# Two transformer layers on one core: one plan for both layers, with shared places in memory

## The chip, the cores and the metric

The kernel runs on one core of a Trainium2 chip. The metric is the device time of one execution, in microseconds (us); it is measured several times, and the median counts.

## The reference

The input is 128 sequences of 64 tokens with 128 features, with a context of the same shape. Two layers follow each other. Layer 0 of the reference is a cross attention with 16 heads and then a routed attention with 8 experts, layer 1 a decoder block and then a mixture of 16 experts:

```python
x = x + _L0_xattn_ref(_layernorm(x), ctx_1024, ...)      # softmax(q k^T / sqrt(8)) v, 16 heads
x = x + _L0_ffn_ref(_layernorm(x), Wr, Wqkv, Wo)         # per expert: top 8 of 64 tokens, rotary q and k, causal softmax
x = x + _L1_xattn_ref(_layernorm(x), ctx_1024, ...)      # self attention, norm, cross attention, norm, relu FFN, norm
x = x + _L1_ffn_ref(_layernorm(x), router_w, bias, ...)  # 4 of 16 experts by group, silu(h) * u, plus 2 shared ones
```

The text below calls the first two lines layer 1 of the kernel, and the last two lines layer 2, as the kernel does ("first_layer", "second_layer"). All is computed in float32.

## The kernel before

The 8192 tokens are cut into 16 chunks of 512 (8 sequences). A chunk lies in SBUF as four tiles of 128 tokens by 128 features, and its transpose as 128 features by 512 tokens, which is one PSUM bank.

Nothing is issued directly. A layer is recorded operation by operation into a `Plan`, by recorders for VectorE (V), ScalarE (A), GpSimd (G), TensorE (T) and the DMA queue of SyncE (Y). `Plan.run` then orders it: it keeps a clock for each engine, takes durations from its own table (`duration`), and always places the operation that can start first, with ties broken by a rank made of the chunk number times a pace, less the length of the work behind it. A chunk may run at most `window` chunks ahead of the oldest unfinished one. Buffers have a tag and a number of slots, and an operation that writes a new buffer has to wait for a slot. In the end all operations are issued in the planned order, so that each engine works strictly through its own list. Almost every instruction carries line 337 (350 after the change), the line that issues them, so a profile is read by the names of tiles.

Before the change there are two plans. `first_layer` opens its pools, records all 16 chunks, runs the plan and closes its pools; then `second_layer` does the same. The two exchange the stream x through DRAM tiles `xm`. Layer 2's weights are fetched when its plan begins. The names that matter:

- Layer 1, each chunk: `x` and `cT` (the context, transposed by the host) come by DMA; LayerNorm gives `z`, TensorE turns it into `zT` (through `tr_ps`); `psk`, `psq`, `psv` are the projections; then an attention in two halves. Each half has sixteen score products `pss`, sums `sc`, a row maximum `mx` that GpSimd subtracts, four transposes `pst`, four exponentials `e` and the products `pso` with the values; `psa` turns the result, `psw` is the output projection.
- Layer 1, each pair of chunks (`routed_attention`): `psl` gives the router's logits, `lg` their sigmoid; they go through DRAM (`logits_d`, `rows`, `rows_d`, `psr`), VectorE ranks them, and one-hot matrices (`hot`, `hotT`) gather (`psg`) and scatter (`psz`) the tokens. At the start the value and output weights of each expert are multiplied into one matrix, `wvo` (the fold: `wvT_ps`, `wvo_ps`).
- Layer 2, each chunk: `decoder_block` has two attentions of the same kind, LayerNorms into z0 to z3, and residual tiles r0 to r3 (`moved` scales and shifts them on GpSimd); `ph` and `po` are the FFN. `expert_layer` routes (`r_psl`, `psc`), sends the combination weights through DRAM so that each partition gets them (`comb_d`, `all_w`), and runs 18 experts: `gate`, `up`, Silu into `mo_g`, times `all_w` on GpSimd, times `up` on VectorE into `mo_a`, and `y`, which accumulates over all experts.

PSUM has eight banks: four ("a") for scores and `pso`, and four ("m") for all else; in layer 2 three of these are "m" and one holds `y`.

Of the kernel before, what the change touches and what calls it, by code (L numbers as in the profile page):

```python
# [25 lines left out]
P = 128  # L26
# [14 lines left out]
PACE1 = 25  # L41
# [22 lines left out]
C_M4, C_BM, C_RK, C_COS, C_SIN, C_TRI, C_R8, C_END = 0, 4, 132, 134, 198, 262, 518, 526  # L64
# [80 lines left out]
class Op:  # L145
    def __init__(self, n, engine, chunk):
        self.n, self.engine, self.chunk = n, engine, chunk
        self.calls, self.us, self.late, self.mode = [], 0.0, 0.1, None
        self.deps, self.then, self.waits, self.ready, self.start, self.end = set(), [], 0, 0.0, 0.0, 0.0
        self.bufs, self.news, self.line_up, self.done = [], [], [], False  # L150


class Plan:
# [3 lines left out]
    def __init__(self, tc, window, prompt=(), pace=0):  # L157


        self.prompt, self.pace = prompt, pace  # L160
        self.tc, self.nc, self.window = tc, tc.nc, window
        self.ops, self.chunk, self.group = [], 0, None
        self.tags, self.turns = {}, {}
        nc = tc.nc
        self.V, self.A, self.G, self.T, self.Y = (
            Recorder(self, e, n) for e, n in ((nc.vector, "V"), (nc.scalar, "A"), (nc.gpsimd, "G"), (nc.tensor, "T"), (nc.sync, "Y"))
        )

    def new(self, pool, shape, name, slots=None, dtype=F32, tag=None, in_turn=False):

        tag = name if tag is None else tag
        slots = pool.slots[tag] if isinstance(pool, Banks) else slots
# [7 lines left out]
    def held(self, tile):  # L180

        return View(Buf(None, list(tile.shape), None, None, 0, None, tile), np.broadcast_to(np.int8(0), list(tile.shape)))
# [20 lines left out]
    def _add(self, calls, us):  # L203
# [22 lines left out]
        for b, reads, writes in seen.values():  # L226
            if reads or writes:
                op.deps.update(b.writers)
            if writes:
# [9 lines left out]
            op.bufs.append(b)  # L239
        op.deps.discard(op)  # L240
# [3 lines left out]
    def free_slots(self, b):  # L244
        return self.tags.setdefault((id(b.pool), b.tag), [0.0] * b.slots)
# [8 lines left out]
    def run(self):  # L254
# [6 lines left out]
        for op in reversed(ops):  # L261
            op.tail = op.us + op.late + max((x.tail for x in op.then if x.chunk == op.chunk), default=0.0)
            op.rank = op.chunk * self.pace - op.tail if self.pace else op.n
# [7 lines left out]
        while done < len(ops):  # L271
# [27 lines left out]
            for b in op.news:  # L299
                slots = self.tags[id(b.pool), b.tag]  # L300
                b.slot = min(range(len(slots)), key=lambda s: slots[s])
                slots[b.slot] = math.inf
# [13 lines left out]
            for b in op.bufs:  # L316
                b.left -= 1
                b.free_at = max(b.free_at, op.end)
                if not b.left and b.slot is not None:
                    self.tags[id(b.pool), b.tag][b.slot] = b.free_at  # L320
            cand[op.engine].remove(op)
            for x in op.then:
                x.ready = max(x.ready, t + us if x.engine == op.engine and op.engine != "Y" else op.end)
# [9 lines left out]
        for op in order:  # L333
            for b in op.news:
                b.real = b.pool.tile(b.shape, b.dtype, name=b.name, tag=f"{b.tag}.{b.slot}", bufs=1)
# [3 lines left out]
        self.ops, self.tags = [], {}  # L339
# [12 lines left out]
def duration(engine, method, out, args, kw):  # L352
# [10 lines left out]
    if engine == "Y":  # L363
        return 0.1, 2.5 + n * out.shadow.shape[0] * 5.0e-6 * 4, None
# [10 lines left out]
    return 0.1 + n * (0.0023 if len(whole) > 1 and min(map(elements, whole)) == n else 0.0019), 0.1, None  # L375

@with_exitstack
def two_layers(ctx: ExitStack, tc: tile.TileContext, a: dict, out: bass.AP):
# [15 lines left out]
    mats = const.tile([P, len(MATS), P], F32, name="mats")  # L394
    nc.scalar.dma_start(out=mats, in_=a["mats"].rearrange("m i o -> i m o"))
    mat = {n: mats[:, i, :] for i, n in enumerate(MATS)}
    rows_t = const.tile([P, len(ROWS), P], F32, name="rows_t")
    nc.scalar.dma_start(out=rows_t, in_=a["rows"].unsqueeze(0).to_broadcast([P, len(ROWS), P]))
    row = {n: rows_t[:, i, :] for i, n in enumerate(ROWS)}
# [12 lines left out]
    def normed(pl, src, sb, affine=False, role="", n=3):  # L412
# [20 lines left out]
        z = pl.new(sb, [P, T, P], "z", n, tag="z" + role)  # L433
# [21 lines left out]
    class Attention:  # L455
# [10 lines left out]
        def __init__(self, pl, pool, ps, n_v, n_kx, s, t, o="o"):  # L466

            one = pool("at1")
            self.pl, self.sb, self.ps, self.n_kx, self.s, self.t, self.o = pl, pool("at2"), ps, n_kx, s, t, o

            v_bd = [one.tile([P, NB, NP, 2 * V1], F32, name=f"v_bd{i}", tag=f"v_bd{i}") for i in range(n_v)]
            for t in v_bd:
                nc.gpsimd.memset(t, 0.0)
                nc.gpsimd.memset(t[:S, :, :, HD : HD + 1], 1.0)
                nc.gpsimd.memset(t[S:, :, :, V1 + HD : V1 + HD + 1], 1.0)
            self.v_bd = [pl.held(t) for t in v_bd]

# [6 lines left out]
        def run(self, c, zT, kvT, w, resid, dst, mask=None, role=""):  # L484
            names = ("Wq", "Wk", "Wv", "Wo") if w == "L0_xattn_" else ("wq", "wk", "wv", "wo")
            wq, wk, wv, wo = (mat[w + n] for n in names)
# [3 lines left out]
            m = lambda shape, name: pl.new(ps, shape, name, tag="m")  # L490
# [31 lines left out]
            for n in range(2):  # L522

                pss = [pl.new(ps, [P, 2, NR, S], "pss", tag=g) for g in self.s]
                sc = [pl.new(sb, [P, 2, NR, S], "sc", 8) for g in range(NR)]
                pst = [pl.new(ps, [P, 4, P], "pst", tag=self.t) for i in range(4)]
                e = [pl.new(sb, [P, 4, P], "e", 4) for i in range(4)]
                pso = pl.new(ps, [P, 2, NH, V1], "pso", tag=self.o)
# [42 lines left out]
                psa = pl.new(ps, [P, 2, P], "psa", tag=self.t)  # L571
# [12 lines left out]
    def biases(m, raw):  # L584
        nc.vector.tensor_copy(m, raw)
        nc.vector.tensor_scalar(m, m, 0.0, NEG, ALU.is_equal, ALU.mult)

    def query_key_mask(pool, src):

        raw = pool.tile([P, S], I32, name="qk_raw")  # L590
        for j in range(2):
            nc.sync.dma_start(out=raw[j * S : (j + 1) * S], in_=src)
        m = pool.tile([P, S], F32, name="qk_m")
        biases(m, raw)
        return lambda t: m.unsqueeze(1).unsqueeze(1).to_broadcast([P, 2, NR, S])

    def key_mask(pl, sb, c, src):
# [6 lines left out]
        pl.V.tensor_copy(m, raw)  # L604
        pl.V.tensor_scalar(m, m, 0.0, NEG, ALU.is_equal, ALU.mult)
# [3 lines left out]
    def first_layer():  # L609

        with ExitStack() as st:
            pool = lambda name, bufs=1, **kw: st.enter_context(tc.tile_pool(name=name, bufs=bufs, **kw))
            one, sb = pool("fl1"), pool("fl2")
            ps = banks(pool, a=4, m=4)
            pl = Plan(tc, 4, prompt="m", pace=PACE1)
            attend = Attention(pl, pool, ps, 2, 2, ("a",) * NR, "m", "a")
            routed = routed_attention(pl, one, sb, ps, pool("fl_d", space=DRAM))
            xs = []
            for c in range(NCH):
                pl.chunk = c  # L620
                xs.append(pl.new(sb, [P, T, P], "x", 6))
                pl.Y.dma_start(out=xs[c], in_=a["x"][c])
                cT = pl.new(sb, [P, CH], "cT", 3)
                pl.Y.dma_start(out=cT, in_=a["ctxT"][c])
                zT = turned(pl, normed(pl, xs[c], sb, n=2), sb, ps, "m")
                pl.G.tensor_tensor(xs[c], xs[c], over_t(row["L0_xattn_bo"]), ALU.add)
                attend.run(c, zT, cT, "L0_xattn_", xs[c], xs[c])
                if c % 2:
                    routed(c - 1, xs[c - 1 :])
            pl.run()  # L630

    def routed_attention(pl, one, sb, ps, dram):
# [9 lines left out]
        wqkv = one.tile([P, E0, 3 * P], F32, name="wqkv")  # L642
        nc.sync.dma_start(out=wqkv, in_=a["L0_ffn_Wqkv"].rearrange("e i j -> i e j"))
        wo = one.tile([P, E0, P], F32, name="ra_wo")
# [447 lines left out]
```

## Time and profile before

| | us |
|---|---|
| median of three runs | 2141.91 (2139.83 to 2142.22) |
| the profiled execution | 2143.89 |
| its span, from first to last instruction | 2142.1 |
| TensorE busy in it | 1947.6 |
| VectorE, ScalarE, GpSimd busy | 1273.5, 1203.7, 1154.8 |
| layer 1's last result stored | 557.2 |
| first product of layer 2 | 580.7 |

The profile comes from one execution under the hardware profiler. Its page has, among other things, each engine's busy time, the span in 40 slices (a digit is the busy share in tenths, and the row PEclk the granted TensorE clock in tenths), and groups of instructions. An answer on a group or a wait can be asked for any stretch of time. A line of a timeline reads: start, duration, engine, line of the kernel, operation, tile written from tiles read, shape, count, and in brackets the idle time before it with what ended it. A wait for several semaphores is put down to the one that came last, which need not be the one that mattered. A float32 matrix product shows as two records.

### The profile page before, as it was taken

The numbers are of one execution on the slowest core, as the hardware profiler recorded it, in microseconds if no ns is written. First come the engines' busy times: TensorE is split into PE (matmuls) and PEld (weight loads), VectorE is DVE, ScalarE is ACT, GpSimd is POOL, SyncE is SP. The second block draws the span as 40 slices with busy tenths as digits, with TensorE's granted clock in tenths as the row PEclk, the third lists the DMA queues.
The fourth block names the chain that finished last, engine by engine and source line by source line (L and its number), as shares of the span: only waits on it lengthen the run. The fifth ranks groups of instructions, "written<-read, shape, count | busy, mean of one in ns | idle before, by whom it ended". The sixth has DMA issues, their size and how long they took to land. (4 is left out here: it accounts for less than half of the span.)

```text
span 2142.1 us, 41746 instructions
## 1 busy us (share of the span) xinstructions
PE 1947.6 (91%) x16032; PEld 1212.7 (57%) x16032; DVE 1273.5 (59%) x3393; ACT 1203.7 (56%) x2147; POOL 1154.8 (54%) x1332
## 2 busy tenths in 40 slices
PE   6988889887388899999999999999999999999999
PEld 4676666665266655555555555555555555555544
DVE  4567767774477846646565665646465665645442
ACT  5867878865245436464655546465555646554322
POOL 5545555643256645646555565656455555644533
PEclk8999999998689889999999999999999999999999
DMA  4011011100400102021111112021111102111131
GB/s 127 9 42 36 20 43 43 43 21 26 136 4 17 51 33 70 28 87 51 58 51 47 51 47 78 21 97 51 47 51 47 63 35 71 51 55 50 49 110 50
DMA packets 62839, 110.77 MB, mean 52 GB/s; under 512 B 17968, under 2 KB 31792, under 8 KB 62640
## 3 DMA queue, kind: packets, MB, share of 16 engines
q1 hardware_dynamic: 58704, 104.69, 14.7%
q10 hardware_dynamic: 3936, 3.41, 0.6%
q8 instruction: 127, 2.08, 0.4%
q14 instruction: 72, 0.59, 0.1%
HBM read 98.37 MB, written 9.70 MB: 50 GB/s over the span
## 5 line engine op out<-in xcount | busy, mean ns | idle before, releaser
L337 POOL TENSOR_TENSOR sc<-sc,mx 128x512 f32<-128x512 f32 x384 | 394.9, 1051 | 338.6 <-DVE mx L337 330.8
L337 POOL TENSOR_TENSOR mo_g<-mo_g,all_w 128x512 f32<-128x512 f32 x256 | 325.0, 1269 | 204.0 <-ACT mo_g L337 203.8
L337 DVE TENSOR_TENSOR mo_a<-mo_g,up 128x512 f32<-128x512 f32 x288 | 196.4, 682 | 305.5 <-PE up L337 275.4
L337 ACT ACTIVATE mo_g<-gate 128x512 f32<-128x512 f32 x288 | 171.5, 596 | 354.7 <-PE gate L337 352.2
L337 PE MATMUL up<-zT,wu 128*128 128x512 f32 x576 | 310.9, 622 | 6.9 <-ACT mo_g L337 6.9
L337 PE MATMUL gate<-zT,wg 128*128 128x512 f32 x576 | 301.6, 606 | 15.9 <-ACT mo_g L337 14.1
L337 ACT ACTIVATE e<-pst 128x512 f32<-128x512 f32 x384 | 219.5, 598 | 168.0 <-PE pst L337 162.2
L337 PE MATMUL y<-mo_a,wd 128*128 128x512 f32 x576 | 299.1, 601 | 0.0
L337 PEld LDWEIGHTS pso<-v_bd,e 128*64 128x64 f32 x6144 | 216.7, 146 | 129.2 <-issue 63.3
L337 PE MATMUL pst<-ident,sc 128*128 128x128 f32 x1536 | 242.9, 296 | 28.6 <-ACT mo_g L337 9.3
L337 DVE TENSOR_REDUCE mx<-sc 128x8 f32<-128x512 f32 x384 | 245.3, 675 | 37.1 <-ACT sc L337 34.1
L337 PE MATMUL pso<-v_bd,e 128*64 128x18 f32 x6144 | 245.5, 219 | 12.2 <-ACT e L337 9.9
L337 ACT ACT_TABLE_LOAD x160 | 205.3, 1283 | 68.5 <-PE pst L337 59.6
L337 PEld LDWEIGHTS pst<-ident,sc 128*128 128x128 f32 x1536 | 183.6, 150 | 82.2 <-issue 27.2
L337 POOL TENSOR_TENSOR ln_rs<-ln_mv,powers 128x4 f32<-128x4 f32 x112 | 61.4, 553 | 213.6 <-DVE ln_mv L337 178.5
L337 PEld LDWEIGHTS gate<-zT,wg 128*128 128x128 f32 x576 | 104.1, 194 | 116.4 <-issue 81.1
L337 PEld LDWEIGHTS y<-mo_a,wd 128*128 128x128 f32 x576 | 101.6, 190 | 96.4 <-issue 94.6
L337 PEld LDWEIGHTS up<-zT,wu 128*128 128x128 f32 x576 | 99.6, 193 | 95.2 <-issue 66.1
L337 DVE RECIPROCAL rc<-pso 128x32 f32<-128x32 f32 x96 | 34.1, 355 | 175.1 <-PE pso L337 174.8
L337 PE MATMUL pss<-kx,q 32*64 32x256 f32 x3072 | 126.2, 413 | 9.5 <-DVE q L337 3.8
L337 ACT ACTIVATE z<-x,ln_off,ln_rs 128x128 f32<-128x128 f32 x256 | 113.1, 487 | 29.5 <-POOL ln_off L337 29.2
L337 DVE TENSOR_TENSOR sc<-pss,qk_m 128x512 f32<-128x512 f32 x128 | 82.3, 683 | 51.6 <-PE pst L337 26.1
(162 smaller groups left out, 2925.3 us busy)
## 6 DMA issues: line engine op xcount, KB each, us to landing
all_w<-comb_d SPq DMA_DIRECT2D x128, 512.0 KB, 4.4
cT<-in_ctxT SPq DMA_DIRECT2D x32, 256.0 KB, 2.7
x<-in_x SPq DMA_DIRECT2D x16, 256.0 KB, 7.5
psr<-rows_d SPq DMA_DIRECT2D x128, 32.0 KB, 2.1
xm<-x SPq DMA_DIRECT2D x16, 256.0 KB, 2.0
x<-xm SPq DMA_DIRECT2D x16, 256.0 KB, 4.0
out<-x SPq DMA_DIRECT2D x16, 256.0 KB, 2.3
k_raw<-in_mask_Bx1x1xS_if SPq DMA_DIRECT2D x32, 64.0 KB, 2.7
```

What stands on the lines that cost most here:

```text
L337: made = getattr(eng, method)(*map(put, args), **{k: put(v) for k, v in kw.items()})
```

## The change

Both layers are now recorded into one plan, over one pool of SBUF tiles and one set of PSUM banks. A table `PLACES` says which place in memory a tag of layer 2 uses: the experts' weights `wg`, `wu`, `wd` take the places of layer 1's `xg` and `wqk`, `mo_g` and `mo_a` those of small tiles of the routed attention, and so on. Some tags have fewer slots: `e` three instead of four, the routed attention's `zT`, `hot`, `scT`, `y` one instead of two; the plan's window is 5 throughout. In the decoder block LayerNorm writes into the tile that it reads (`dst=r`), `moved` works in place, and one tag `r` with four places carries the stream through all stages, where nine tiles (z0 to z3, r0 twice, r1 to r3) did before.

What holds layer 2 back is written out. Each of its operations gets 100 added to its rank (`BEHIND`). `marks` remembers operations of layer 1: the two first decoders may begin once the logits of pair six (counted from zero) have been sent to DRAM, those of chunks 2 to 5 once the last pair's have; the experts' weights follow the last gather of layer 1. The first four matrices and the first row are fetched at once, the other eight and nine with layer 2's weights, all now on SyncE's queue, and the routed attention's weights come after the first two chunks' x. `duration` charges a DMA 0.4 us on the queue instead of 0.1.

The diff, cut to its core:

```diff
-PACE1 = 25
+BEHIND = 100
+EARLY = 6
+WINDOW = 5
...
-            op.rank = op.chunk * self.pace - op.tail if self.pace else op.n
+            op.rank = op.chunk * self.pace - op.tail + op.behind if self.pace else op.n
...
-        return 0.1, 2.5 + n * out.shadow.shape[0] * 5.0e-6 * 4, None
+        return 0.4, 2.2 + n * out.shadow.shape[0] * 5.0e-6 * 4, None
...
+PLACES = {
+    "kx0": ["kx.0"], "kx1": ["kx.1"], "q0": ["q.0"], "q1": ["q.1"], "aT0": ["aT.0"], "aT1": ["aT.1"],
+    "zT0": ["zT.0"], "zT1": ["zT.1"], "zT2": ["psr.0"], "qk_raw": ["k_raw.0"],
+    "r": ["r.0", "r.1", "lg.0", "lg.1"], "h0": ["rot.0"], "h1": ["rot.1"],
+    "z4": ["hotT1.0"], "zT4": ["zr.0", "zr.1"], "yT": ["hotT0.0"], "comb": ["zTr.0"],
+    "mo_g": ["y.0", "ra_v.0", "ra_v.1"], "mo_a": ["scT.0", "rsc.0", "rsc.1"],
+    "all_w": ["trig.0", "xp.0", "wvo.0", "sw.0", "sw.1"],
+    "wg": ["xg.0"], "wu": ["xg.1"], "wd": ["wqk.0"],
+    "m2": ["m.0", "m.1", "m.2"], "py": ["m.3"],
+}
...
-                e = [pl.new(sb, [P, 4, P], "e", 4) for i in range(4)]
+                e = [pl.new(sb, [P, 4, P], "e", 3) for i in range(4)]
...
+            marks[pl.chunk // 2] = {pl.ops[-1]}
...
+                marks[-1] = {pl.ops[-1]}
...
-        def moved(zn, gamma, shift, role):
-
-            r = pl.new(sb, [P, T, P], "r", 1, tag="r" + role)
-            pl.G.tensor_tensor(r, zn, over_t(gamma), ALU.mult)
-            pl.G.tensor_tensor(r, r, over_t(shift), ALU.add)
-            return r
+        def again(r, role, g):
+
+            normed(pl, r, sb, affine=True, role=role, dst=r)
+            return turned(pl, r, sb, ps, "m2", col["L1_xattn_g" + g], col["L1_xattn_b" + g], role=role, n=1)
+
+        def moved(r, g):
+            pl.G.tensor_tensor(r, r, over_t(row(pl, "L1_xattn_g" + g)), ALU.mult)
+            pl.G.tensor_tensor(r, r, over_t(row(pl, "L1_xattn_b" + g)), ALU.add)
...
         def run(c, x):
-            zT = turned(pl, normed(pl, x, sb, role="4", n=1), sb, ps, "m", role="4")
+            pl.after = set(last)
+            zT = turned(pl, normed(pl, x, sb, role="4", n=1), sb, ps, "m2", role="4")
+            pl.after = set()
             all_w = route(zT)
...
-    first_layer()
-    second_layer()
...
+    pl = Plan(tc, WINDOW, prompt=("m", "m2"), pace=25, places=PLACES)
+    attend = Attention(pl, sb, ps, 2, 2)
...
+    for c in range(NCH):
+        pl.chunk = c
+        x, cT = loaded(c, a["x"][c])
+        xs.append(x)
+        zT = turned(pl, normed(pl, x, sb, n=2), sb, ps, "m")
+        pl.G.tensor_tensor(x, x, over_t(row(pl, "L0_xattn_bo")), ALU.add)
+        attend.run(c, zT, cT, "L0_xattn_", x, x)
+        if c == 1:
+            routed = routed_attention(pl, sb, ps, dram)
+        if c % 2:
+            routed(c - 1, xs[c - 1 :])
+
+    for c in range(NCH):
+        pl.chunk = NCH + c
+        pl.behind = BEHIND
+        if c == 0:
+            the_rest(pl)
+            decoder = decoder_block(pl, sb, ps, attend)
+            pl.after = marks[-1]
+            experts = expert_layer(pl, sb, dram, ps)
+            pl.after = set()
+        x, cT = loaded(c, pl.held(x_mid[c]))
+        pl.after = marks[EARLY if c < 2 else NCH // 2 - 1] if c <= WINDOW else set()
+        decoder(c, x, cT)
+        pl.after = set()
+        experts(c, x)
+    pl.run()
```

## The prediction

> **What bounds the kernel now.** I read the page's shares first, then the busy times by stage, then TensorE's (PE's) waits stage by stage, and last the timeline around the largest waits.
>
> ```profile
> PE 1947.6 (91%) x16032; PEld 1212.7 (57%) x16032; DVE 1273.5 (59%) x3393; ACT 1203.7 (56%) x2147; POOL 1154.8 (54%) x1332
> ...
> PE   6988889887388899999999999999999999999999
> ...
> PEclk8999999998689889999999999999999999999999
> ```
>
> PE is the only engine near its span, but not evenly: slice 10 has a hole. The busy times by stage (length; PE, weight loads, VectorE, ScalarE, GpSimd; then the granted clock) show where it is idle and where its clock is low:
>
> ```profile
> 0.00:26.00 26.00, 9.89 (x46) 7.72 (x46) 7.65 (x45) 6.67 (x13) 8.49 (x23) 1.00 0.82 258
> 26.00:120.00 94.00, 84.97 (x988) 58.97 (x989) 53.30 (x121) 77.69 (x154) 54.43 (x71) 0.84 0.05 12
> 120.00:450.00 330.00, 291.47 (x3488) 227.69 (x3487) 244.14 (x571) 262.22 (x508) 186.87 (x223) 0.96 0.12 36
> 450.00:557.00 107.00, 77.04 (x697) 60.60 (x696) 57.31 (x125) 54.16 (x97) 36.75 (x42) 0.82 0.08 23
> 557.00:740.50 183.50, 141.41 (x1680) 101.54 (x1679) 120.69 (x329) 85.62 (x174) 96.09 (x123) 0.85 0.17 49
> 740.50:1900.00 1159.50, 1108.90 (x8219) 638.81 (x8217) 687.47 (x1908) 632.56 (x1060) 656.23 (x739) 0.97 0.16 55
> ```
>
> From 740 us on PE is busy 96% of the time at clock 0.97: that stage is bound by PE. From 450 to 740 us it is idle 65.7 us (107.0 − 77.0 + 183.5 − 141.4) and runs at 0.82 to 0.85. The waits say why: in the stage from 456 us on
>
> ```profile
> PE psk L337 <- DMA k_raw<-in_mask_Bx1x1xS_if: 23.4, 1, 23.4
> PE rankT_ps L337 <- DVE rows L337: 6.6, 2, 6.2
> PE psg L337 <- DVE hotT L337: 5.2, 2, 4.0
> ```
>
> layer 1's last pair of chunks goes through its routing alone, and then layer 2's first product waits for data and weights. In the PE-bound stage the waits are short and always the same:
>
> ```profile
> PE gate L337 <- ACT mo_g L337: 14.1, 12, 1.2
> PE pst L337 <- ACT mo_g L337: 8.6, 11, 0.8
> PE psk L337 <- DVE zT L337: 8.2, 11, 0.8
> ```
>
> The start, from the timeline: the fold of layer 1's weights stands first on PE and waits 14.4 us for its data, and the first chunk's transposes come at 26 us.
>
> ```profile
> 14.40 1.94 PE L337 MATMUL wvT_ps<-ident,wqkv 128*128 128x128 f32 x8 [14.40 <-DMA wqkv<-in_L_ffn_Wqkv]
> ...
> 26.36 0.90 PE L337 MATMUL tr_ps<-ident,z 128*128 128x128 f32 x3 [0.51 <-ACT v_bd L337]
> ```
>
> **What the Trainium skill says.** "TensorE: Matmul & The Clock Gate", section "What's actually happening": PE's clock is halved after an idle window of about 3.4 us and restored after a busy one, and the windows run on by themselves. The trace agrees, though waits of 2.0 us in all were enough (the timeline and one stretch's busy times, clock 0.55):
>
> ```profile
> 1324.66 1.12 PE L337 MATMUL gate<-zT,wg 128*128 128x512 f32 x2 [1.18 <-ACT mo_g L337]
> 1326.57 1.94 PE L337 MATMUL pst<-ident,sc 128*128 128x128 f32 x8 [0.78 <-ACT mo_g L337]
> ...
> 1326.00:1331.00 5.00, 4.43 (x26) 3.01 (x26) 2.13 (x10) 2.90 (x4) 4.63 (x6) 0.55 0.39 116
> ```
>
> Such dips come 191 us apart, with every second chunk: the stores of finished chunks are alternately 93.7 and 97.6 us apart, so a dip costs 3.9 us. "ScalarE: Activation LUTs", section "What ACT_TABLE_LOAD costs", gives about 1283 ns for the load and more for a drain; the trace has 1283 ns for the mean of 160 loads and shows no drain after them. "Trainium Kernel Development and Optimization", section "Performance Expectations", calls matmul busy time a bad measure because matmuls are pipelined. I therefore count PE work by pitch (start to start, full clock) from the dense timeline: 0.86 us for a 128x512 product, 0.9 for four 128x128 products, 0.44 for four transposes, 0.55 for eight pso products, 1.0 for sixteen pss, 3.55 for po. Over the whole program that gives 1742 us, the same for both kernels: the built program after has the same 9208 matmuls.
>
> **The change, part by part.** I take five stages, marked by events on PE that both programs have, with the PE work that each program's own instruction order puts before them.
>
> Start to the last psz of the first pair. Before: 94.5 us of work by 149.2 us. After, x and cT of the first chunks stand ahead of the 2 MB for the fold, so LayerNorm runs while weights come. But PE issues in order, and its fourth product needs the third chunk's cT, whose DMA follows the fold's weights: 4.4 MB are ahead of its end. Before moved 4.4 MB in about 14.3 us, so I put that product at 15 us and the transposes at 16.5 instead of 26.4: 10 us won. About 2 us of it go to the fold, which now stands between the chunks. Mark at 149.2 − 8.5 = 140.7 us (bounds: 4 and 11 us won).
>
> To the last psz of the sixth pair (of eight). Before: 231.3 us of work in 300.5 us, so 0.770 per us. After: 236.7 us of work, as some of the next pair's is drawn ahead. Layer 1 has three places instead of four for e and one instead of two or three for zT, scT, y, hot; ScalarE, busy 79% here, gets two more table loads, 2.6 us. I take the same rate: 307.4 us (0.75 would give 316).
>
> To the last psz of layer 1. Before: 58.4 us of work in 107.5, a chain of routing, DMAs and softmax with nothing beside it. After: 83.9 us, since decoder work of layer 2's first two chunks stands between. The chain itself can't get shorter than its 107 us by much. I take 112 us (rate 0.75), 105 if decoder work only fills waits, 125 if it delays the chain. On the SP queue 1.7 MB for layer 2 (mats, rows, w12) now stand ahead of one pair's rank row; at the start's rate of 0.31 MB per us that delays one routing by up to 5 us, covered by the other chunks' attention, and it is inside these bounds. The experts' 3.5 MB come after the last pair's psr and before its results are stored; they land while decoders run.
>
> To the point from which PE's order is the same in both (the psq before the first experts' stream). Before: 111.1 us of work in 183.3, with the 23.4 us hole. After: 80.5 us is left. Before's decoder-only stretch, 599.7 to 739.7 us, did 103.0 us of work in 140.0, rate 0.736. At this rate 109.4 us (103 at 0.78, 118 at 0.68). Four r places now cap the chunks in flight, where r and z had nine tiles.
>
> The rest. PE's work per chunk is 84.9 us in both. Before took 1401.5 us. What is new there: three e places, so that the built ScalarE order splits one group of four exponentials and has twelve table loads per chunk instead of ten. I walked through that place with the durations above. Before, from the end of the last y to the second psa, 10.2 us of PE work took 13.8. After, the three gates are followed by pst, a wait of 1.2 us for load and first e, and later one of 2.3 us for the fourth e (mo_g 0.6 between two loads of 1.28): 10.1 us of work in 13.7. The new wait takes the place of the old ones. In place LayerNorm makes moved (1.27 us per GpSimd pass, as before) wait for the transposes; its result is needed only at psw, an attention later. Without that cover each of three passes would cost 2.5 us a chunk. I take 1401.5 (−27 to +37: clock dips that vanish or double, below).
>
> Sum: 140.7 + 307.4 + 112 + 109.4 + 1401.5 = 2071.0 us against 149.2 + 300.5 + 107.5 + 183.3 + 1401.5 = 2142.0, the profiled span of 2142.1. That execution took 2143.89 and the runs' median is 2141.91, so span and median are the same within 0.01% and I carry nothing over. Prediction 2071.
>
> **Rivals.** (1) The joint is not filled: the chain of the last pair is delayed to 125 us, decoders run at 0.68, layer 1 at 0.75. That is +13, +9 and +9: 2087 to 2110. For it: waits in the decoder stage are on VectorE and ScalarE, not on PE. Against: after has two kinds of work to choose from. 17 in 100. (2) The stream of experts gets slower: the clock dips come with every chunk instead of every second (six more at 3.9 us, +23), and the two loads per chunk expose up to 1 us more (+14 over 14 chunks): 2090 to 2125. For it: one wait is now 2.3 us long without a break. 12 in 100. (3) The other way: the waits are split so that no window is idle enough, and half or all of the dips go: 12 to 27 us less, 2044 to 2059. 13 in 100. (4) Slower than before: the third e place. If in each of the 96 half attentions (16 chunks, three attentions, two halves) the fourth exponential waits for the first pso to read its tile and PE stands behind it, 0.74 us each eats the whole 71 us; from there on the kernel is slower. Before's waits of PE's pso on e in the long stage are 4.5 us in all, and the pso of the first e is through 0.8 us after it while two more exponentials take 1.2. 4 in 100. (5) The start does not move, because PE's in-order fold and the third cT decide: +8, inside the main case. That the overlap isn't there is excluded: the order has 30.6 us of layer 2 work before layer 1's last psz.
>
> **How the numbers follow.** The main case, 2059 to 2087, has 52 in 100; with the four rivals (17, 12, 13, 4), 1 for no change and 1 below 2044 that is all. The predicted time is the main case's. From 2047 to 2106 lie the main case, 14 of rival 1's 17, 11 of rival 3's 13 and 5 of rival 2's 12: 82 in 100. A difference under 0.2%, 4 us, is about what can't be told from none. Faster 0.95, same 0.01, slower 0.04.
>
> **What would show it.** PE's slice row has no hole at 550 us and the clock row no run of low digits there; the first tr_ps stands near 16.5 us; gate, up and y run densely by 672 us instead of 742; chunks leave every 95 to 96 us as now. A prediction too low would show dips after each chunk or PE waits on e; one too high, dips gone.

## The result, and the profile after

The kernel after takes 2152.7 us (median of nine runs, 2147.4 to 2162.0) against 2141.8 before: a ratio of 1.0059, interval 1.0042 to 1.0077. It is slower, by some 11 us, where 71 us less was forecast. Its profiled execution took 2152.14 us, its span 2150.3. Medians in this text are over all runs of a kernel, while the ratios leave out three single runs in a slower state (one each with a fourth e, with four separate h and with r alone).

The page of the kernel after (engine totals, TensorE's busy row and its clock row):

```profile
PE 1959.2 (91%) x16032; PEld 1199.0 (56%) x16032; DVE 1295.8 (60%) x3390; ACT 1235.5 (57%) x2172; POOL 1156.2 (54%) x1326
...
PE   6888998899898989898999899999999898999999
...
PEclk9899989999889999999999999999999999999999
```

The hole between the layers (a 3 in the row before) is gone, but where the row had nines to the end there are now some eights. The busy times by stage say the same (columns as before: length; TensorE (PE), weight loads, VectorE, ScalarE, GpSimd; granted clock):

```profile
120.00:450.00 330.00, 289.63 (x3329) 222.92 (x3330) 231.21 (x543) 260.21 (x492) 179.41 (x213) 0.93 0.13 40
450.00:557.00 107.00, 97.76 (x1108) 75.84 (x1106) 86.40 (x219) 84.35 (x164) 64.36 (x77) 0.95 0.24 72
557.00:740.50 183.50, 167.54 (x1756) 116.66 (x1762) 138.30 (x376) 94.87 (x179) 113.81 (x136) 0.93 0.12 39
740.50:1900.00 1159.50, 1072.49 (x7825) 596.68 (x7810) 669.18 (x1777) 627.51 (x1029) 619.56 (x695) 0.96 0.15 52
```

From 450 to 740 us PE is busy 265.3 us instead of 218.5: the joint is filled as intended. After 740 us it is busy 1072.5 of 1159.5 us instead of 1108.9, so the time is given back there. At the five marks of the prediction (the column "before" as the prediction has it; read at the ends of the products, as for the kernel after, its second and third numbers are 300.0 and 108.0):

| stage | before | predicted | after |
|---|---|---|---|
| start to first pair's last psz | 149.2 | 140.7 | 151.4 |
| to sixth pair's last psz | 300.5 | 307.4 | 318.3 |
| to the last psz of layer 1 | 107.5 | 112.0 | 114.2 |
| to the psq ahead of the experts' stream | 183.3 | 109.4 | 105.3 |
| the rest | 1401.5 | 1401.5 | 1461.1 |

The rest divides further by the stores of finished chunks. The first comes 103.9 us into it (110.8 before), the twelfth 1116.7 us later (1049.7 before), and what follows takes 240.4 (241.0). The first finished chunk thus leaves 58 us earlier than before (793.1 against 851.4), and the eleven steady intervals lose more than that: they take 101.5 us a chunk instead of 95.4, 67 us in all. PE's waits from 770 to 1900 us (waiting tile, tile waited for, us in total, times, longest):

```profile
PE pso L350 <- ACT e L350: 35.5, 34, 1.8
PE psk L350 <- DVE zT L350: 21.2, 11, 2.0
PE pst L350 <- ACT e L350: 19.0, 11, 1.7
```

The waits for e over the same stretch in the kernel before:

```profile
PE pso L337 <- ACT e L337: 4.5, 6, 0.8
PE pst L337 <- ACT e L337: 2.6, 12, 0.6
```

The largest entry before was 14.1 us; the waits for e have grown from 7.1 to 54.5 us. Each chunk now has three waits of some 1.7 to 2.0 us (timeline of PE):

```profile
1413.59 0.93 PE L350 MATMUL pso<-v_bd,e 128*64 128x18 f32 x16 [1.77 <-ACT e L350]
...
1441.35 1.12 PE L350 MATMUL psk<-zT,mats 128*128 128x512 f32 x2 [2.00 <-DVE zT L350]
...
1477.48 0.63 PE L350 MATMUL pst<-ident,sc 128*128 128x128 f32 x4 [1.73 <-ACT e L350]
```

After the first, the granted clock is 0.68 in the five microseconds from 1414:

```profile
1414.00:1419.00 5.00, 5.00 (x21) 2.78 (x20) 1.89 (x6) 2.94 (x6) 0.00 (x0) 0.68 0.26 101
```

From 1000 to 1900 us there are 17 such dips, about two a chunk, each just after one of the three waits (seven times that of pso, five times each of the others); before had five, longer ones. In these 900 us PE is idle for 68.3 instead of 38.5 us, and 31.5 instead of 20.0 us of its busy time are lost to the clock (busy time times what the granted clock lacks of 1). At 101.5 and 95.4 us a chunk that is 7.7 instead of 4.1 us idle and 3.6 instead of 2.1 us lost in each, together 5.1 of the 6.1 us.

### The profile page after: what moved, and what is told of

Its sections match the earlier page's. It is cut to its first block, busy times and chain, and to the rows that moved or that the text cites. A ratio compares the mean times of both kernels' runs of the same rounds, so it can differ in the third digit from the quotient of the medians.

```text
span 2150.3 us, 41561 instructions
## 1 busy us (share of the span) xinstructions
PE 1959.2 (91%) x16032; PEld 1199.0 (56%) x16032; DVE 1295.8 (60%) x3390; ACT 1235.5 (57%) x2172; POOL 1156.2 (54%) x1326
## 4 chain that ended last, share of the span: by engine, by line
PE 58%; ACT 20%; DVE 8%; POOL 6%; issue 6%; SPq 2%; DMA 1%; ACTq 0%; DVEq 0%; POOLq 0%
PE py L350 10%; PE up L350 9%; PE gate L350 8%; PE pso L350 7%; ACT L350 6%; PE pst L350 5%; PE pss L350 3%; ACT e L350 3%; PE po L350 3%; ACT mo_g L350 2%; POOL mo_g L350 2%; PE psv L350 2%; PE psq L350 2%; POOL ln_rs L350 2%; SPq L350 2%
## 5 line engine op out<-in xcount | busy, mean ns | idle before, releaser
L350 PE MATMUL gate<-zT,wg 128*128 128x512 f32 x576 | 306.1, 617 | 10.4 <-ACT mo_g L350 7.0
L350 PE MATMUL py<-mo_a,wd 128*128 128x512 f32 x576 | 312.5, 625 | 0.0
L350 PEld LDWEIGHTS pst<-ident,sc 128*128 128x128 f32 x1536 | 175.3, 145 | 114.9 <-issue 54.1
L350 PEld LDWEIGHTS gate<-zT,wg 128*128 128x128 f32 x576 | 100.5, 195 | 111.5 <-issue 68.3
L350 PEld LDWEIGHTS up<-zT,wu 128*128 128x128 f32 x576 | 103.6, 199 | 93.3 <-issue 65.7
L350 POOL TENSOR_TENSOR r<-r,rows_t 128x512 f32<-128x512 f32 x112 | 141.9, 1267 | 24.0 <-PE tr_ps L350 14.3
L350 PEld LDWEIGHTS py<-mo_a,wd 128*128 128x128 f32 x576 | 103.0, 197 | 85.5 <-issue 83.7
L350 PE MATMUL pss<-kx,q 32*64 32x256 f32 x3072 | 121.7, 398 | 3.4 <-DVE at L350 2.7
L350 ACT COPY v_bd<-psv 64x256 f32<-64x256 f32 x192 | 74.2, 386 | 66.8 <-PE psv L350 64.8
```

Source lines behind the costliest of these rows:

```text
L350: made = getattr(eng, method)(*map(put, args), **{k: put(v) for k, v in kw.items()})
```

## The experiments

There are three theories. **e**: PE waits because e has three places instead of four. **r**: PE waits because the decoder stream works in place in four tiles. **order**: the joint plan has settled into another sequence (its ScalarE order has 12 table loads a chunk instead of 10), and no tile is to blame. "Spacing" below is the mean of the eleven steady intervals in the profiled execution. The median of the runs and the ratio to before stand with it. The diffs show the core of each edit, and of the longer lines of `PLACES` the changed part.

**A fourth e in layer 2 of the kernel after** (z.0 is used by layer 1 alone):

```diff
-                e = [pl.new(sb, [P, 4, P], "e", 3) for i in range(4)]
+                e = [pl.new(sb, [P, 4, P], "e", 3, tag="e" if bank == "m" else "e2") for i in range(4)]
+    "e2": ["e.0", "e.1", "e.2", "z.0"],
```

> The kernel after, with a fourth place for e in layer 2 (z.0, which only layer 1 uses). Nothing else is changed; its ScalarE order still has 12 table loads per chunk in the steady stream, as the kernel after. Theory 'third e place' (PE waits 28.5 us for e before pso and 15.5 before pst in nine steady chunks because an exponential has no place): these waits go back to under 8 us, chunks leave every 95 to 97 us instead of 101.5, and the whole takes 2085 to 2100 us. Rival 'order' (the planner has settled into another sequence for each chunk, with two more table loads, and places are not the cause): chunks still 100 to 102 us apart, 2140 to 2155 us.

Spacing 99.9, median 2156.0 (1.0058, 1.004 to 1.0076). The fourth e gives 1.6 us a chunk, not 6; pso and pst still wait 39.5 us for e in nine chunks. The whole gains nothing, since this execution reached the end of layer 1 at 596.1 us instead of 583.9, although PE's order up to there is the same instruction by instruction, and its first chunk left at 824.7 instead of 793.1. The clock makes this difference, not waits: between the first and the sixth pair PE is idle for 39.1 us (38.7 in the kernel after), but loses 31.8 us of busy time to the clock (18.4); from layer 1's end to the first chunk it is idle for 17.4 us (15.1) and loses 26.9 (8.3). Layer 1 in the joint plan thus varies by 12 us between executions, and smaller differences in it aren't read below. Neither theory holds alone.

**One zT4** (the expectation calls this the number of before; that is an error, before has two as well):

```diff
-    "z4": ["hotT1.0"], "zT4": ["zr.0", "zr.1"],
+    "z4": ["hotT1.0"], "zT4": ["zr.0"],
```

> The kernel after, with one place for the experts' input zT4 instead of two (the number that the kernel before has). e keeps three places and r four. The built ScalarE order has 10 table loads per chunk again. Theory 'order': what is lost per chunk is the two table loads and the waits at them, so chunks leave every 95 to 97 us and the whole takes 2085 to 2105 us. Theory 'third e place': nothing comes back, 2145 to 2160 us, with PE's waits for e as long as after's (44 us in nine steady chunks).

Spacing 109.0, 2283.6 us (1.0659). Ten table loads a chunk, and 131 us slower than after: the number of loads says nothing by itself. zT4 is read by all 18 experts of a chunk; with one place the next chunk's router can't begin until they are through, and PE's largest wait from 1000 to 1900 us is now one for the router's comb (23.5 us in nine chunks).

**Four separate h** instead of two of double size:

```diff
+    "h2": ["hot.0"], "h3": ["gated.0"],
...
-                if f % 2 == 0:
-                    hh = pl.new(sb, [P, 2, CH], "h", tag=f"h{f // 2}")
...
-                h.append(hh[:, f % 2])
+                h.append(pl.new(sb, [P, CH], "h", tag=f"h{f}"))
```

> The kernel after, with four separate places for the FFN's hidden tiles h (as in the kernel before) instead of two of double size; e three, r four, zT4 two places. This order too has 10 table loads per chunk. Theory 'order': the same gain as with one zT4, 2085 to 2105 us, although a different resource is touched. Theory 'third e place': 2145 to 2160 us.

Spacing 100.65, 2150.6 us (1.0037, 1.0018 to 1.0057). Ten loads again, but little gained. "Order" in the form expected here falls, as the loads go and the loss stays. The waits are others, with nearly all of pst for e gone (2.3 us):

```profile
PE psk L350 <- DVE zT L350: 37.7, 11, 3.6
PE pso L350 <- ACT e L350: 17.1, 11, 1.6
```

**Both scarcities in the kernel before**, then each alone. This is the core of the edit for r (normed writes into dst, as in the change) and the one for e:

```diff
-            r = pl.new(sb, [P, T, P], "r", 2, tag="r0")
+            r = pl.new(sb, [P, T, P], "r", 4)
+            normed(pl, x, sb, role="0", dst=r)
...
-            r = moved(z, row["L1_xattn_g1"], shift[:, 0], "1")
+            moved(r, row["L1_xattn_g1"], shift[:, 0])
...
-                e = [pl.new(sb, [P, 4, P], "e", 4) for i in range(4)]
+                e = [pl.new(sb, [P, 4, P], "e", 3) for i in range(4)]
```

> The kernel before, with the decoder stream in place in four r tiles and with three places for e in both layers: the two scarcities of the change without the joint plan. Its order has 10 table loads per chunk, as before's. Theory 'third e place' (or the in-place stream): slower than before by 40 us or more, in both layers. Theory 'order': within 10 us of before, 2133 to 2152 us.

Spacing 100.7 (before 95.4), first finished chunk at 886.9 us (851.4), 2235.7 us (1.0438, 1.0418 to 1.0458). The two tile cuts, without the joint plan, cost 94 us; PE's steady order is that of the kernel after with four h, but for one product into y a chunk that stands elsewhere.

> The kernel before with the in-place decoder stream alone: r in four tiles, where z0 to z3 and five r tiles were nine; e keeps four places. Before with both scarcities lost 94 us (its finished chunks 100.7 us apart instead of 95.4, and its first finished chunk 35 us later). Theory 'four r tiles' (the next decoder can't begin LayerNorm until a tile of the stream is free, so zT comes late and PE waits before psk): chunks 99 to 101 us apart, first chunk late by 25 us or more, 2205 to 2240 us. Theory 'third e place': chunks within 1 us of before's 95.4, 2138 to 2150 us. If the two add, about half each: 2170 to 2200 us.

r alone has a spacing of 98.5, first chunk at 874.9, 2215.1 us (1.0323, 1.0271 to 1.0374; the profiled execution, of 2201 us, is the fastest of these). PE's wait for zT before psk from 1000 to 1900 us is 29.5 us (6.7 in the kernel before).

> The kernel before with three places for e (both layers) and its nine tiles for z and r. Theory 'third e place': chunks 99 to 101 us apart, 2190 to 2240 us. Theory 'four r tiles': 2138 to 2152 us, waits of PE for e in the steady stream under 10 us in nine chunks.

e alone has a spacing of 97.2, first chunk at 849.1, 2167.4 us (1.0138, 1.0105 to 1.017). PE, ScalarE and VectorE have exactly before's order of tiles in the steady stream; what grows is PE's waits of pso for e, from 3.8 to 12.6 us. In the spacing the two add: 3.1 and 1.8 make 4.9 of the 5.3 us a chunk.

**Giving them back to layer 2 of the kernel after.** First z0 to z3 stand apart from the four r again, in places of layer 1; then there is a fourth e besides. The core of the first edit:

```diff
+    "z0": ["z.0"], "z1": ["hot.0"], "z2": ["psr.1"], "z3": ["z.1"],
...
-            moved(r, "1")
+            r = moved(z, "1")
```

> The kernel after, with LayerNorm's results in tiles of their own again (z0 to z3, in places that only layer 1 uses) beside the four r tiles: eight tiles for the decoder stream. e keeps three places. Theory 'four r tiles': chunks 95 to 97.5 us apart instead of 101.5, 2085 to 2110 us. Theory 'third e place': 100 to 102 us apart, 2135 to 2160 us.

Spacing 98.8, 2139.6 us (0.9993, 0.9977 to 1.0009). The wait for zT before psk is gone.

> The kernel after, with both given back to layer 2: eight tiles for the decoder stream and four places for e. If the two scarcities are all that the steady stream lost, whatever their shares, chunks leave 95 to 97 us apart and the whole takes 2080 to 2100 us. If the order in which the joint plan happens to settle is the cause (12 table loads per chunk are still there), 99 to 102 us apart and 2125 to 2155 us.

Spacing 97.6, 2121.3 us (0.9925, 0.9899 to 0.9952): faster than before, with 2.1 us a chunk still missing.

**All of layer 2's tiles as before.** The first version also took away one of zT4's two places, both of which before has.

> The kernel after, with all of layer 2's tiles as before: z0 to z3 apart from the four r, four e, four separate h, one zT4, each in a place that only layer 1 uses. The joint plan, the start and layer 1 stay. With stream and e alone given back, chunks still left 97.6 us apart with 12 table loads each; this order has 10. Theory 'scarce tiles' (the rest of the 2.1 us per chunk is tiles too): 95.2 to 96 us apart, 2092 to 2110 us. Theory 'the joint plan's own order' (rank, DMA price, held tiles): 97 to 98 us apart, 2115 to 2132 us.

Its spacing was 98.1, but its last three intervals were 62.7, 62.0 and 59.9 us where they are 57.2, 49.9 and 45.1 in the kernel after, and it took 2164.2 us (1.0112, 1.0084 to 1.0139). The next version has zT4's two places, h2 in gated.1, h3 in x.5 and, as before's layer 2, five x:

```diff
+    "h2": ["gated.1"], "h3": ["x.5"],
+    "z0": ["z.0"], "z1": ["hot.0"], "z2": ["psr.1"], "z3": ["z.1"],
+    "e2": ["e.0", "e.1", "e.2", "gated.0"], "x2": ["x.0", "x.1", "x.2", "x.3", "x.4"],
```

> The kernel after, with layer 2's tiles as before: z0 to z3 apart from four r, four e, four separate h, five x, and zT4 with its two places (a_full had taken one of them away by mistake, which is what made its last chunks slow). The rules of the joint plan, the start and layer 1 stay as after. TensorE's built order in the steady stream is now the same as before's, instruction by instruction. Theory 'tiles': chunks 95.2 to 95.8 us apart, first finished chunk at 800 to 825 us, the whole 2090 to 2112 us. Theory 'the joint plan costs something of its own': 97 us apart or more, over 2115 us.

Spacing 94.6, **2102.1 us (0.982, 0.979 to 0.985)**: faster than both kernels, with every rule of the joint plan, its start and its layer 1 kept. PE, ScalarE and, but for one small operation a chunk, VectorE have before's sequence again. PE's waits from 770 us to the twelfth store (1858 us):

```profile
PE gate L350 <- ACT mo_g L350: 14.1, 12, 1.2
...
PE psk L350 <- DVE zT L350: 8.5, 11, 0.8
PE pso L350 <- ACT e L350: 7.0, 10, 0.8
...
PE pst L350 <- ACT e L350: 2.3, 12, 0.2
```

These are before's, to within 2.5 us. So the steady loss is tiles, not the joint plan's rules. The last 3 us a chunk (97.6 to 94.6; 94.9 in the two kernels that follow) came with the h tiles: paired, they go with a sequence with two more table loads and the wait of pst for e. (x has one place fewer here, which wasn't tried by itself.) The early part does not keep all that the kernel after won: its first chunk leaves at 816.8 us, 24 us after that kernel's and 35 before before's, with PE between layer 1's end and that chunk idle for 22.3 us (15.1 in the kernel after) and 20.8 us (8.3) lost to the clock.

**What the overlap is worth.** This is the same kernel, with every decoder held until layer 1's last result is stored:

```diff
+    done = {pl.ops[-1]}
...
-        pl.after = marks[EARLY if c < 2 else NCH // 2 - 1] if c <= WINDOW else set()
+        pl.after = done if c <= WINDOW else set()
```

> The same, but no decoder may begin before layer 1's last result is stored (weights and x still come early). This takes the overlap of compute away and nothing else. If the overlap is worth what the prediction gave to the joint (107.5 + 183.3 us before, 112 + 109.4 predicted, a gain of 69 us less 7 of work moved ahead), the whole is 45 to 70 us slower than the version with overlap, 2140 to 2175 us. If most of the gain is the weights that are there already when layer 2 begins, less than 25 us slower. Chunks 95.2 to 95.8 us apart in any case.

2135.8 us (0.9971), 33.7 us slower; spacing 94.9. Its layer 1 ends at 572.3 us and its first chunk leaves at 850.7, 278 us later, where before took 294 (557.4 to 851.4). So overlapped compute gives 34 us. The 16 us are what PE is idle less between layer 1's end and the first chunk (33.4 us instead of 49.1), where before waits 23.4 us for data; that early data and weights give them is likely, but they weren't held back by themselves. The overlap also has a price: from the sixth pair to layer 1's end this kernel takes 95.0 us, and with overlap 107.2. Starting the overlap a pair earlier (`EARLY = 5`):

> The same as the first, but the two first decoders may begin one pair earlier (after the logits of pair five instead of six). Layer 1 is bound by its scarce tiles there, not by PE, so PE has room: 2 to 10 us less than the first, 2085 to 2105 us, if decoder work fills waits; equal or slower by up to 10 us if it delays layer 1's chains.

2099.5 us (0.9796, 0.9761 to 0.9832): no difference that can be told.

**Layer 1's tiles.** Before, with the routed attention's fewer places alone:

```diff
-            z = [normed(pl, x, sb, role="r", n=3) for x in xs]
-            zT = [turned(pl, t, sb, ps, "m", role="r") for t in z]
+            z = [normed(pl, x, sb, role="r", n=2) for x in xs]
+            zT = [turned(pl, t, sb, ps, "m", role="r", n=1) for t in z]
...
-                hot = ns([P, 4, 2, S], "hot")
+                hot = ns([P, 4, 2, S], "hot", 1)
...
-                scT = ns([P, 4, P], "scT")
+                scT = ns([P, 4, P], "scT", 1)
...
-                y = ns([P, 4, P], "y")
+                y = ns([P, 4, P], "y", 1)
```

> The kernel before with the routed attention's fewer places alone: hot, scT, y and its zT one instead of two, its z two instead of three; layer 2 untouched. Theory 'scarce places slow layer 1' (the kernel after needs 318 us from the first to the sixth pair's last psz, before 300): sixth pair's last psz at 458 to 466 us instead of 449.3, layer 1 ends at 565 to 575 instead of 557.4, the whole 2148 to 2162 us. Rival (it is the order of the joint plan): within 4 us of before at all three.

The first pair is done at 148.5, the sixth at 460.9 (312.3 us between them instead of 300.0), layer 1 at 572.0 (557.4 before), and the whole takes 2159.7 us (1.0089, 1.0064 to 1.0114); the spacing is 95.43, as before. The fewer places of the routed attention cost layer 1 some 12 to 15 us. Between the two marks PE is idle for 41.6 us (35.5 before) and loses 21.4 us of busy time to the clock (11.4). The third e may add to this: in the two kernels before with three e the same stretch takes 303.3 and 311.6 us, though PE's order in it is the same, and again the clock differs (10.2 and 20.1 us lost).

**The start.** The fold's weights become work of chunk 2, so that four x and three cT go first:

```diff
+            pl.chunk = 2
             routed = routed_attention(pl, sb, ps, dram)
+            pl.chunk = 1
```

> The kernel after with the start's edit alone. Theory 'third cT': the first tr_ps on PE at 15 to 18 us instead of 22.8, first pair's last psz at 141 to 147 us instead of 151.4, the whole 2140 to 2148 us. Rival (the start is bound by ScalarE's and GpSimd's attention work, whatever PE gets first): first pair's last psz at 149 to 153 us, 2148 to 2156 us. The steady stream isn't touched: chunks 101 to 102 us apart.

The first tr_ps came at 16.47 us instead of 22.83, and the first pair's last psz at 150.2 instead of 151.4; the whole took 2173.3 us (1.0144; layer 1 ended at 601.8). The same edit on the first version with all tiles:

> The kernel before this one, and besides the fold's weights are recorded as work of chunk 2, so that the third and fourth chunk's x and cT are fetched before the 2 MB of layer 1's weights. If the start's loss comes from PE's fourth product waiting for the third cT behind those weights, the first pair's last psz is at 141 to 147 us instead of 151 to 154, and the whole 5 to 9 us below the kernel without this edit: 2085 to 2104 us. If layer 1's own rate decides, the gain is gone by the sixth pair: within 4 us of it.

The first tr_ps came at 16.1 us and the first pair's last psz at 148.0; the whole took 2189.3 us. Early transposes hardly move the first pair, and both kernels are slower for the edit. What does set the first pair's time stays open.

**Why zT is late.** In the kernel after, GpSimd's and VectorE's timelines just ahead of the 2.00 us wait:

```profile
1437.94 2.60 POOL L350 TENSOR_TENSOR r<-r,rows_t 128x512 f32<-128x512 f32 x2
...
1438.02 1.27 DVE L350 TENSOR_TENSOR g_gt<-g_gt,g_eq 128x64 f32<-128x64 f32 x1 [0.28 <-POOL g_eq L350]
1439.32 0.22 DVE L350 TENSOR_REDUCE g_r<-g_gt 128x16 f32<-128x64 f32 x1
1439.58 1.00 DVE L350 TENSOR_SCALAR g_r<-g_r 128x16 f32<-128x16 f32 x1
1440.49 0.80 DVE L350 TENSOR_SCALAR zT<-tr_ps,vec 128x512 f32<-128x512 f32 x1
```

Two operations on 64 and 16 elements, g_gt<-g_gt,g_eq and g_r<-g_r, which take 0.225 and 0.175 us in the kernel before, take 1.27 and 1.00 here and end as GpSimd's passes over r end; the copy of zT is queued behind them. "SBUF — State Buffer" of the Trainium skill, section "Who interferes with whom", says that VectorE and GpSimd share one pair of ports, that a VectorE operation with two SBUF inputs or in a two-port mode contends with GpSimd for it, and that the loser is blocked for the other's whole instruction. The trace agrees: g_gt, with two inputs in SBUF, is held, and the reduction, with one, is not (0.22 us). Whether g_r's operation is in a two-port mode no trace shows; that it is held fits. In the kernel before with r in place the same thing happens at another spot of the router. Groups from 1000 to 1900 us (after the bar: busy us, mean ns), in the kernel before and then in that one:

```profile
L337 DVE TENSOR_SCALAR tot<-tot 128x4 f32<-128x4 f32 x18 | 3.1, 170 | 0.6
...
L337 DVE TENSOR_TENSOR w<-w,tot 128x64 f32<-128x64 f32 x9 | 2.0, 224 | 0.3
```

```profile
L337 DVE TENSOR_SCALAR tot<-tot 128x4 f32<-128x4 f32 x20 | 18.4, 922 | 0.7
L337 DVE TENSOR_TENSOR w<-w,tot 128x64 f32<-128x64 f32 x10 | 12.4, 1242 | 0.3
```

To tell this from the number of r tiles, the passes over r are made on one of each token's 128 features, with every order kept; the other features are left unscaled and unshifted:

```diff
+                if op.engine == "G" and args[0].buf.name == "r" and len(args) == 4:
+                    args = (*(put(v)[:, :, 0:1] for v in args[:3]), args[3])
```

> The kernel before with the in-place stream, but GpSimd's passes over r (scale, shift and output bias of the decoder's stream) are issued on one of 128 features only, so they take some 0.2 us instead of 1.27; the other features are left unscaled and unshifted. All engines' orders, tiles and waits are the same as with full passes. Theory 'GpSimd's passes hold the router's small VectorE operations': tot and w<-w,tot at 170 to 400 ns, PE's wait for zT before psk under 12 us in nine to ten chunks instead of 29.5, chunks 95.3 to 96.3 us apart instead of 98.5. Theory 'four r tiles hold the next decoder back': the wait stays over 20 us, chunks 97.5 us apart or more.

In the kernel before with r in place: spacing 94.2 instead of 98.5, 2147.6 us (1.0023) instead of 2215.1; PE's wait for zT is 8.2 us instead of 29.5, w<-w,tot takes 225 ns again (tot 584, as every second one still runs beside a GpSimd pass over mo_g). PE's wait, with full and with thin passes:

```profile
PE psk L337 <- DVE zT L337: 29.5, 10, 3.6
```

```profile
PE psk L339 <- DVE zT L339: 8.2, 10, 0.8
```

The first chunk stays late, 873.7 us: that part isn't the passes. Four tiles for the decoders that run alone there would explain it, but that wasn't tried by itself.

> The same cut in the kernel after. Theory 'GpSimd's passes': g_gt and g_r at 180 to 400 ns instead of 1272 and 1001, the wait for zT before psk under 6 us instead of 17.2, chunks 98.3 to 99.6 us apart instead of 101.5 (as with separate tiles, 98.8), 2112 to 2132 us; PE's waits for e stay at 40 us or more in nine chunks. Theory 'four r tiles': chunks over 100.5 us apart, 2140 to 2155 us.

In the kernel after: spacing 98.1 instead of 101.5, 2117.2 us (0.989, 0.9856 to 0.9924), g_gt at 225 and g_r at 174 ns, the wait for zT gone, and the waits for e as they were (30.2 and 15.5 us in nine chunks). The passes over r, where the in-place stream puts them, are what makes zT late. The thin passes also give GpSimd itself some of its time back, but separate tiles with full passes removed the same wait.

## Why the prediction was wrong

**The rest: 1401.5 predicted, 1461.1 measured.** This is the step that failed, and the sign with it: the prediction put the change's price in the steady stream at nothing, and it is 6.1 us a chunk. Three things make it up (their sum is a little more, as the stream with all tiles is itself 0.5 to 0.9 us shorter than before's).

- *"In place LayerNorm makes moved wait for the transposes; its result is needed only at psw."* True of the result, but a pass was costed only by who needs its output. It also holds some of VectorE's small operations while it runs, and its later place is beside the router, ahead of zT. Measured 2.7 us a chunk (separate tiles) to 3.4 (thin passes).
- *"The new wait takes the place of the old ones."* One spot was walked, with 1.2 and 2.3 us of waits; the trace has 0.75 and 1.77 there, and PE's waits for mo_g did shrink from 29.2 to 6.4 us (770 to 1900 us), so that walk was about right. But exponentials and experts meet again some 60 us later in the chunk, where pst waits 1.73; that second spot was not walked. The missing e is worth 1.2 to 1.8 us a chunk.
- The double-size h was not priced at all. With it the plan has the two extra loads and that second wait, which stays when a fourth e is given (17.3 us from 1000 to 1900 us) and goes when h is four tiles; without it, stream and e being back, 2.7 to 3.0 us a chunk return.

**The start: 140.7 predicted, 151.4 measured.** The third cT came at 17.7 us (15 predicted), and the transposes at 22.8 (16.5), as PE waited for VectorE's kx besides. But the step fails further on: with transposes at 16.5 the mark is still 150.2. An earlier start of PE was taken as won at the mark; it isn't. This is rival 5's outcome, though not its reason: it put it on the fold and the third cT, and with these out of the way the mark stays.

**To the sixth pair: 307.4 predicted, 318.3 measured.** "The same rate" failed: 0.744 per us instead of 0.770. Of the 18 us more than before, 8 are more work (7 were forecast, for work drawn ahead), 3 are idle time of PE and 7 are lost to the clock. The fewer places alone cost 12 us between the same marks in the kernel before; the bound given for 0.75, 316, was the better value. Even so this execution was a good one: ten other kernels with the same order of PE up to this mark took 319.8 to 330.5 us. How much the third e and how much the joint plan add to the 12 us stays open.

**The joint: right, in part by luck.** 112 and 109.4 were predicted and 114.2 and 105.3 measured, with the mechanism named: there is no hole, and no wait of PE from 557 to 690 us is longer than 1.6 us. But the reason given for 112, that the chain can't get much shorter than its 107 us, doesn't hold: with the decoders held back it takes 95.0 (with 5 us of its work drawn ahead), so decoder work does delay it. And the clock was kind to this execution (8.3 us lost from layer 1's end to the first chunk, where the one with a fourth e loses 26.9). The idle time quoted for the joint, 65.7 us, is a slip: the four figures give 72.1. No term rests on it. The cap of four r doesn't show there.

**Rivals.** Rival 2 came, with its dips at every chunk and PE waits on e, but at nearly twice its upper price (67 us instead of 37), and mostly for causes that it didn't name. Rival 4 had the right place for e, not the size: it asked for 71 us, and the third e costs 26 us in the kernel before and, in layer 2 of the kernel after with the stream separate, 18. No rival had GpSimd's passes.

## What to carry to other kernels

An edit that saves memory by working in place moves operations, and a moved GpSimd pass can be paid for by small VectorE operations that it now runs beside and by whatever is queued behind those: look at what VectorE does at the new place before calling the pass hidden. When a change joins stages by taking tiles away, price the tiles in the steady stage first: here 6.1 us a chunk in eleven intervals outweighed the 58 us won before. A place that is free in one of the two layers (six were here) can give the tile back at no cost in memory, which made 2152.7 us 2102.1.

## What the hardware showed that was not expected

Two of VectorE's operations, on 4 and 64 elements per partition, take over five times as long where a 1.27 us GpSimd pass runs beside them (170 to 922 ns, 224 to 1242), while a reduction of 64 elements beside such a pass is not held (220 ns). And a single wait of PE of 1.5 to 2.0 us was followed by a stretch at a lower clock about twice in each chunk, so a wait can cost more than its length. In the kernel before with r in place, where PE's waits for zT last up to 3.6 us, thin passes took the clock loss from 1000 to 1900 us from 24.2 us to none.
